# Moving the rare tiles' branch, the split of gathered tiles and two small turns in a convolution, attention and expert kernel

## The chip, the cores and the metric

The kernel runs on one core of a Trainium2 chip. The metric is the device time of one execution in microseconds; lower is better. A profile of one execution tells what each engine did: TensorE (PE, with its weight loads as PEld), VectorE (DVE), ScalarE (ACT), GpSimd (POOL) and SyncE (SP), which only issues transfers here. A letter q behind an engine's name (PEldq, POOLq) means its instruction queue: register loads, branches, semaphore instructions.

## The reference, cut to what matters

Two layers on an image of 256 channels and 48 x 48 pixels, 2304 tokens:

```python
x = x + _L0_conv_ref(_gn(x), ...)         # group norm, q, k, v, full softmax attention over 4 * 2304 rows
t = _to_tokens(x)                         # 2304 tokens of 256 channels
t = t + _L1_attn_ref(_ln_t(t), ...)       # attention over 64 slices
t = t + _L1_ffn_ref(_ln_t(t), ...)        # experts, below
x = _from_tokens(t, x)

def _L1_ffn_ref(x, Wg, bg, W1, b1, W2, b2):
    gate_logits = xf @ Wg + bg
    top_w, top_i = jax.lax.top_k(gate_logits, 2)
    top_w = jax.nn.softmax(top_w, axis=-1)
    w_dense = ...                          # weight of each of 8 experts for each token, two of them not zero
    for e in range(8):
        h = jax.nn.gelu(xf @ W1[e] + b1[e], approximate=False)   # 256 -> 1024
        out = out + w_dense[:, e:e + 1] * (h @ W2[e] + b2[e])    # 1024 -> 256
    return out
```

All of it is float32.

## The kernel before, in words

The first layer opens with the weights' turns, the group norm and the projections (lines 247 to 360); its attention over 9216 rows takes most of the time, up to about 1215 us. The change doesn't touch it. Two places are touched: the first 17 us, and the expert stage from about 1278 us on.

**The start.** Weights are turned on TensorE into PSUM tiles `pw` (two of them in turn, pool `ps_w`) and copied out by ScalarE. VectorE computes mean and variance of the channels; TensorE spreads them over groups with a small matrix (`gm`) into a PSUM tile `pgb`. `busy_first(n)` issues n matmuls without a use[...]; they write another part of the same tile `pgb`. `spread()` issues the second group matmul (the variance) and turns all biases (`brow`, 78 rows) into `pb`, which is a part of `pgb` again. VectorE then copies `pb` to `bcol` and scales the query's bias to `bq8`. The norm of five blocks of tokens (TBLOCKS) and their projections follow (`pq`, `pk` from a pool of five PSUM tiles `pp`).

**Routing.** The gate gives each token two experts. The (token, expert) pairs are sorted by expert into tiles of 128 rows: 36 tiles are always there (`SURE`), up to 7 more by how the experts' counts are rounded up: tiles 36 to 38 are "near" ones, 39 to 42 (from `FAR` on) are "rare" ones. `slot_t` holds for each tile the row of each slot, `part_t` the same for quarters of rows. `used_i` is the number of tiles in use. For the inputs here tiles 36, 37 and 38 run, and no rare tile does: 39 tiles of work are in the profile (1248 matmuls `ph`, 32 a tile). At the end of routing `busy(8, spin)` issues eight fillers on TensorE.

**A tile's work.** GpSimd gathers its 128 rows from memory with an indirect transfer: whole rows (`rows`, one transfer, into `xs`) or in four parts of 64 columns (`parts`, four transfers). A tile in rows is turned by TensorE and copied by VectorE (`turn`); a tile in parts needs no TensorE, VectorE turns it in two instructions (`turn_parts`). `first(s)` multiplies by W1 (32 matmuls into PSUM tiles `ph`, three in turn) and ScalarE puts Gelu into `hid`. `second(s)` multiplies by W2 (16 matmuls into `py`), VectorE adds the bias and scales by the token's weight (`y`), and `scatter(s)` adds the rows to `t_d` in memory, again by GpSimd. SyncE loads W1 of the tile's expert, 1 MB (`load_w1`, two buffers). All of W2 stays on the chip. In the trace `w` is W1 and `w_sb` W2.

**Order.** The order on each engine is made when the kernel is built: a scheduler takes what its model holds ready, in the order of the program. An `If` is one block: what stands inside is not mixed with what stands outside. In the program's order:

1. gathers of the near tiles and of tiles 0 and 1, W1 of tiles 36 and 37;
2. the value `used` is loaded on every engine, and the nested `If`s of the rare tiles (lines 1350 and 1355) follow; all are jumped over here;
3. tile 36, then tiles 37 and 38, each in an `If` (line 1386) that is entered here;
4. the loop over the 36 sure tiles: first(s), gather and load of tile s + 2, second(s - 1) with the turn of tile s + 1 in its middle, scatter(s - 1). At s = 4 `judge` computes whether the attention's sums stayed in range (its flag decides at the end whether everything runs again), with a turn on TensorE into `pm`.
5. the last sure tile isn't scattered, but added while the result is turned and stored.

Where an `If` is jumped over, each engine runs a few semaphore instructions that stand in for what was left out.

Lines that matter: `spread` (293), `busy(8, spin)` (1202), `ring_xs` (1220), `in_parts` (1254), `parts` (1257), `turn` (1278), the rare tiles (1354 to 1360), `judge` (1367), the near tiles (1382 to 1392), the loop (1395 to 1420).

Of the kernel before, what the change touches and what calls it, by code (L numbers as in the profile page):

```python
# [9 lines left out]
FP = mybir.dt.float32  # L10
# [55 lines left out]
def layers(  # L66
# [181 lines left out]
    with proj, tc.tile_pool(name="ps_pj", bufs=5, space=PSUM) as ps_pj, tc.tile_pool(  # L248
# [11 lines left out]
            nc.scalar.copy(dst, pw)  # L260
            return dst

        pgb = ps_g.tile([P, 512], FP, name="pgb")

        def busy_first(n):
            for _ in range(n):
                pe.matmul(
                    pgb[:, 256:512], ones, ones.unsqueeze(1).to_broadcast([P, 2, P]), start=True, stop=True
                )

        busy_first(14)
        WqT = transposed(pj.tile([P, 2, C], FP, name="WqT"), raws["Wq"])
        pg = pgb[:, 0:4].rearrange("p (a b) -> p a b", a=2)
        pb = pgb[:, 16:94]

        st = pj.tile([P, 2, 6, 6], FP, name="st")
        mv = pj.tile([P, 2, 2], FP, name="mv")
# [12 lines left out]
        mean = pj.tile([P, 2], FP, name="mean")  # L290
        dve.tensor_copy(mean, pg[:, 0, :])

        def spread():
            pe.matmul(pg[:, 1, :], gm, dm, start=True, stop=True)
            pe.transpose(pb, brow, ident[0:78, 0:78])

        busy_first(2)
        spread()
        WkT = transposed(pj.tile([P, 2, C], FP, name="WkT"), raws["Wk"])
        rstd = pj.tile([P, 2], FP, name="rstd")  # L300
        rsqrt(rstd, pg[:, 1, :], 1e-5, 2)
        xn = t_flat[:, 0 : 2 * NT].rearrange("p (c n) -> p c n", c=2)
        dve.tensor_copy(bcol, pb)
        bq8 = pj.tile([P, 2], FP, name="bq8")
        dve.tensor_scalar(bq8, bcol[:, B_Q : B_Q + 2], 0.125, None, ALU.mult)
        WvT = transposed(pj.tile([P, 2, C], FP, name="WvT"), raws["Wv"])

        for bi, (t0, tn) in enumerate(TBLOCKS):
            toks = slice(t0, t0 + tn)
            for c in range(2):  # L310
                nc.vector.tensor_scalar(
                    xn[:, c, toks], x_sb[:, c, toks], mean[:, c : c + 1], rstd[:, c : c + 1],
                    ALU.subtract, ALU.mult,
                )
            for m in range(2):
                cols = slice(m * P, (m + 1) * P)
                pq = ps_pj.tile([P, 512], FP, name="pp", tag="pp")
                pk = ps_pj.tile([P, 512], FP, name="pp", tag="pp")
                for c in range(2):
                    nc.tensor.matmul(  # L320
                        pq[:, 0:tn], WqT[:, c, cols], xn[:, c, toks], start=(c == 0), stop=(c == 1)
                    )
# [727 lines left out]
    with gating, tc.tile_pool(name="onehot", bufs=1) as oh, tc.tile_pool(  # L1050
# [148 lines left out]
                pq[:, k, :], quad[:, k, :, :].rearrange("p q s -> p (q s)"), empties, start=True, stop=True,  # L1199
            )  # L1200
        dve.tensor_scalar(part_t, pq, 4.0, quarter, ALU.mult, ALU.add)
        busy(8, spin)

    def expert_of(s, engine):
        return nc.values_load(
# [5 lines left out]
    with tc.tile_pool(name="ps_h", bufs=1, space=PSUM) as ps_h, tc.tile_pool(  # L1211
# [5 lines left out]
        def ring(pool, n, shape, name):  # L1217
            return cycle([pool.tile(shape, FP, name=f"{name}{k}") for k in range(n)])

        ring_xs, ring_w1 = ring(fp, 2, [P, C], "xs"), ring(fp, 2, [P, 2, HID], "w1")  # L1220
        ring_xT, ring_hid = ring(fp, 3, [P, 2, P], "xT"), ring(fp, 2, [P, NHC, P], "hid")
        ring_y = ring(fp, 2, [P, C], "y")
        ring_ph, ring_py = ring(ps_h, 3, [P, 4, P], "ph"), ring(ps_y, 2, [P, C], "py")
# [2 lines left out]
        near_xs = iter([fp.tile([P, C], FP, name=f"near_xs{s}") for s in range(SURE, FAR)])  # L1226
        fin = ctx.enter_context(tc.tile_pool(name="fin", bufs=1))
        far_xs, far_w1 = fin.tile([P, C], FP, name="far_xs"), fin.tile([P, 2, HID], FP, name="far_w1")
        here = fin.tile([P, NT], FP, name="here")
        held = fin.tile([P, NTT], FP, name="held")  # L1230
        obs = cycle([fin.tile([P, 2, 512], FP, name=f"ob{k}") for k in range(3)])
# [20 lines left out]
            return xs  # L1252

        def in_parts(s):
            return 2 <= s < SURE and s % 4 != 1

        def parts(s, xs):

# [16 lines left out]
            )  # L1275
            return w1

        def turn(xs):

            pt = next(ring_pt)  # L1280
            for c in range(2):
                pe.transpose(pt[:, c, :], xs.rearrange("p (d c) -> p c d", c=2)[:, c], ident)
            xT = next(ring_xT)
            dve.tensor_copy(xT, pt)
            return xT

# [7 lines left out]
                )  # L1294
            return xT

        def first(s, xT, w1):

            e = expert_of(s, mybir.EngineType.Activation)
            hid = next(ring_hid)  # L1300
# [12 lines left out]
            return hid  # L1313
# [32 lines left out]
            xs[s] = rows(s, next(near_xs))  # L1346
        for s in range(2):
            w1[SURE + s] = load_w1(SURE + s, next(ring_w1))
            xs[s] = parts(s, next(ring_xs))
        used = nc.values_load(  # L1350
            used_i, min_val=0, max_val=NSL,
            skip_runtime_bounds_check_because="it is a sum of counts, cut at NSL",
        )

        with ExitStack() as more:
            for s in range(FAR, NSL):
                more.enter_context(tc.If(used > s))
                issued.clear()
                far = turn(rows(s, far_xs))
                scatter(s, second(s, first(s, far, load_w1(s, far_w1)), lambda: None))  # L1360
        issued.clear()

        def turn_next(s):
            if s in xs:
                xT[s] = (turn_parts if in_parts(s) else turn)(xs.pop(s))
# [1 line left out]
        def judge():  # L1367

            both = fp.tile([P, 2], FP, name="both", tag="judge")
            dve.tensor_reduce(both, ends_of, AX.X, ALU.max)  # L1370
            dve.tensor_scalar(both[:, 0:1], both[:, 0:1], HIGH, None, ALU.is_gt)
            dve.tensor_scalar(both[:, 1:2], both[:, 1:2], 1.0 / LOW, None, ALU.is_gt)
            dve.tensor_tensor(both[:, 0:1], both[:, 0:1], both[:, 1:2], ALU.max)
            pm = ps_j.tile([1, P], FP, name="pm")
            pe.transpose(pm, both[:, 0:1], ident)
            dve.tensor_reduce(bad, pm, AX.X, ALU.max)
# [6 lines left out]
        hid[SURE] = first(SURE, xT.pop(SURE), w1.pop(SURE))  # L1383
        w1[SURE + 2] = load_w1(SURE + 2, next(ring_w1))
        scatter(SURE, second(SURE, hid.pop(SURE), more_turns))
        with ExitStack() as more:
            for s in near[1:]:
                more.enter_context(tc.If(used > s))
                issued.clear()
                hid[s] = first(s, xT.pop(s), w1.pop(s))  # L1390
                scatter(s, second(s, hid.pop(s), lambda: turn_next(s + 1) if s + 1 in near else None))
        issued.clear()
        for s in range(2):
            w1[s] = load_w1(s, next(ring_w1))
        for s in range(SURE):
            hid[s] = first(s, xT.pop(s), w1.pop(s))
            if s + 2 < SURE:
                xs[s + 2], w1[s + 2] = parts(s + 2, next(ring_xs)), load_w1(s + 2, next(ring_w1))
            if s == 0:
                turn_next(1)  # L1400
            elif s < SURE - 2:
                scatter(s - 1, second(s - 1, hid.pop(s - 1), lambda: turn_next(s + 1)))
            if SURE - 3 <= s < SURE - 1:

                scatter(s, second(s, hid.pop(s), lambda: turn_next(s + 1) if s == SURE - 2 else None))
            if s == 4 and bad is not None:
                judge()
            if s == 6:
                dve.tensor_scalar(
                    held, lim[:, 0:NTT], -1.0, empties[:, SURE - 1 : SURE], ALU.mult, ALU.add  # L1410
# [105 lines left out]
```

## Time and profile before

| what | value |
|---|---|
| time, three runs | 1590.86 us median (1588.08, 1590.86, 1597.04) |
| the profiled execution | 1584.99 us |
| its span, first to last instruction | 1583.3 us |
| mean granted TensorE clock | 0.997 |
| gathers in parts | 104 issues (26 tiles of 4), 1.01 us each on GpSimd |
| gathers in rows | 10 issues for sure tiles, 3 for near ones |
| scatters | 38 issues, 1.62 us each |
| W1 of one tile | 3.57 us on the chain of waits |
| W2 of one tile | 3.46 us |
| copies `xT<-pt` behind a TensorE turn | 13, 0.42 us each |

How to read it: "busy" is the time in which an engine executes; a wait is the idle time in front of an instruction, put down to what ended last before it. On TensorE a matmul in float32 is recorded as two instructions, and the recorded ends of neighbouring matmuls overlap, so distances between starts are taken for the time of a group. The time of an instruction on GpSimd's row is the time to issue a transfer; the data land later. Stretches list for each engine the busy time, and the granted clock of TensorE (1.00 is full speed).

### The profile page before, as it was taken

Reading aid. Unit: us, or ns where it says so; the run is one execution under the profiler, and the core shown is the slowest. Engines: PE = TensorE matmul, PEld = TensorE weight load, DVE = VectorE, ACT = ScalarE, POOL = GpSimd, SP = SyncE. Lnnn points to the kernel's source line nnn. Section 1 sums busy time; section 2 is a strip of 40 time slices with the busy share of each in tenths; the row PEclk is TensorE's granted clock in tenths of the full one; section 3 lists DMA queues with packets and bytes.
Section 4 is the critical chain, followed back from the end, with each engine's and each line's share of the span. In section 5 each row is a group of like instructions: output and inputs, shape, how many; then the busy total and the mean of one; then the engine's idle time right before and its main releaser. Section 6 shows DMA issues by size and latency. Waiting matters only on the chain. (4 is left out here: it accounts for less than half of the span.)

```text
span 1583.3 us, 32306 instructions
## 1 busy us (share of the span) xinstructions
PE 1562.8 (99%) x13105; PEld 781.2 (49%) x13105; DVE 1038.1 (66%) x1323; ACT 830.9 (52%) x1168; POOL 270.0 (17%) x210
## 2 busy tenths in 40 slices
PE   9999999999999999999999999999999999999998
PEld 5633343333333333333333333333334689999996
DVE  7578787787777778878778778787787731211111
ACT  2256565565666556656656566566655433333331
POOL 0001001011010010110101101101010135767671
PEclk9999999999999999999999999999999999999999
DMA  4000000000000000000000000000000946666665
GB/s 137 1 1 1 1 1 3 7 1 1 9 1 1 8 1 2 7 2 2 4 5 1 2 8 1 1 8 1 1 2 14 337 141 194 195 185 183 190 180 162
DMA packets 53071, 79.32 MB, mean 50 GB/s; under 512 B 22719, under 2 KB 43406, under 8 KB 47790
## 3 DMA queue, kind: packets, MB, share of 16 engines
q1 hardware_dynamic: 42834, 66.45, 12.7%
q0 software_dynamic: 9424, 10.10, 3.7%
q8 instruction: 108, 1.77, 0.4%
q10 hardware_dynamic: 652, 0.56, 0.1%
q14 instruction: 53, 0.43, 0.1%
HBM read 62.94 MB, written 12.32 MB: 48 GB/s over the span
## 5 line engine op out<-in xcount | busy, mean ns | idle before, releaser
L60 ACT ACTIVATE p<-s 128x1024 f32<-128x1024 f32 x648 | 663.3, 1024 | 470.4 <-PE s L60 465.2
L60 DVE TENSOR_TENSOR acc<-acc,p 128x1024 f32<-128x1024 f32 x612 | 749.3, 1224 | 243.4 <-ACT p L60 237.4
L60 PE MATMUL av<-p,v_sb 64*64 64x512 f32 x5184 | 675.7, 590 | 2.4 <-ACT p L60 1.3
L60 PE MATMUL s<-q,kk 64*64 64x512 f32 x5184 | 674.7, 589 | 0.5 <-DVE tn L60 0.5
L60 PEld LDWEIGHTS s<-q,kk 64*64 64x64 f32 x5184 | 202.0, 133 | 353.6 <-issue 181.5
L60 PEld LDWEIGHTS av<-p,v_sb 64*64 64x64 f32 x5184 | 195.6, 131 | 357.9 <-ACT p L60 201.0
L60 POOL PARTITION_ALL_REDUCE total<-both x17 | 71.1, 4185 | 1011.5 <-ACT p L60 833.6
L60 ACT ACTIVATE hid<-ph,bcol 128x128 f32<-128x128 f32 x312 | 89.3, 368 | 197.5 <-PE ph L60 185.2
L60 PEld LDWEIGHTS ph<-xT,w 128*128 128x128 f32 x1248 | 146.9, 194 | 2.7 <-issue 0.7
L60 PE MATMUL ph<-xT,w 128*128 128x128 f32 x1248 | 147.3, 277 | 0.6 <-issue 0.6
L60 PE MATMUL py<-w_sb,hid 128*128 x624 | 142.8, 379 | 0.0
L60 PEld LDWEIGHTS py<-w_sb,hid 128*128 128x128 f32 x624 | 114.9, 190 | 13.6
L1237 POOL DMA_INDIRECT xs<-tn_d,part_t x104 | 106.2, 1021 | 39.2 <-issue 30.8
L60 DVE TENSOR_TENSOR y<-py,b_bc 128x256 f32<-128x256 f32 x39 | 16.6, 425 | 126.2 <-PE py L60 126.2
L1237 POOL DMA_INDIRECT t_d<-y,slot_t x38 | 61.6, 1620 | 56.9 <-DVE y L60 37.9
L60 DVE STREAM_TRANSPOSE xT<-xs 128x128 f32<-128x128 f32 x52 | 13.1, 290 | 51.0 <-DMA xs<-tn_d,part_t 51.0
L60 DVE COPY xT<-pt 128x256 f32<-128x256 f32 x13 | 5.4, 424 | 53.1 <-PE pt L60 53.1
L60 DVE RECIPROCAL rinv<-rinv 128x256 f32<-128x256 f32 x17 | 29.7, 1745 | 0.0
L60 POOL TENSOR_TENSOR rstd_t<-ve,mhalf 128x2 f32<-128x2 f32 (+2 forms) x13 | 11.0, 849 | 102.8 <-DVE ve L60 96.0
L60 DVE TENSOR_TENSOR acc<-p 128x1024 f32<-128x1024 f32 x18 | 22.1, 1225 | 4.9 <-ACT p L60 3.3
L337 DVE TENSOR_SCALAR q<-pp,bcol 64x512 f32<-64x512 f32 (+1 forms) x30 | 20.8, 694 | 6.2 <-PE pp L320 5.8
L60 DVE TENSOR_REDUCE up<-av 128x512 f32<-128x1024 f32 x17 | 20.8, 1225 | 5.0 <-PE av L60 5.0
(302 smaller groups left out, 620.4 us busy)
## 6 DMA issues: line engine op xcount, KB each, us to landing
w<-in_L_ffn_W_dram SPq DMA_DIRECT2D x39, 1024.0 KB, 6.5
w_sb<-in_L_ffn_W_dram SPq DMA_DIRECT2D x8, 1024.0 KB, 10.2
t_sb<-turned SPq DMA_DIRECT2D x224, 8.0 KB, 1.8
x_sb<-in_x_dram SPq DMA_DIRECT2D x3, 576.0 KB, 3.8
xs<-tn_d,part_t POOLq DMA_INDIRECT x104
t_d<-t_sb SPq DMA_DIRECT2D x2, 768.0 KB, 10.7
tn_d<-tn SPq DMA_DIRECT2D x2, 768.0 KB, 5.7
t_sb<-t_d SPq DMA_DIRECT2D x3, 512.0 KB, 4.6
```

What stands on the lines that cost most here:

```text
L60: return self.tc.keep_in_program_order(getattr(self.engine, name)(*args, **kwargs))
L337: nc.vector.tensor_scalar(dst, pq[rows, 0:tn], bcol[rows, B_Q + m : B_Q + m + 1], 0.125, ALU.add, ALU.mult,)
L1237: new = nc.gpsimd.indirect_dma_start(**kwargs)
```

## The change

In neutral words:

- Start: the fillers get a PSUM tile of their own (`spun`, one of the five `pp`), `pgb` shrinks to 96 columns; the turn of the biases, the copy `bcol` and `bq8` move from before the norm to behind the norm of the first block, into a `pw` tile.
- The fillers at the end of routing go from 8 to 6.
- Tiles in parts: s % 3 < 2 instead of s % 4 != 1, for 2 <= s < 36.
- `ring_xs` has three buffers instead of two; tiles 0, 1 and 2 are gathered ahead, and the loop gathers tile s + 3. Tiles are turned two ahead (s + 2): a TensorE turn in the middle of second(s - 1), a turn in parts behind it, before the scatter.
- The rare tiles' nested `If`s move from before tile 36 into the loop, behind second(0) and scatter(0) at s = 1; they get `hid` and `xT` tiles of their own. The load of `used` moves behind tile 36.
- `judge` is split: VectorE's part stays at s = 4, the turn and the flag (`verdict`) come at s = 5.

```diff
-        pgb = ps_g.tile([P, 512], FP, name="pgb")
+        pgb = ps_g.tile([P, 96], FP, name="pgb")
+        spun = ps_pj.tile([P, 512], FP, name="pp", tag="pp")
...
                 pe.matmul(
-                    pgb[:, 256:512], ones, ones.unsqueeze(1).to_broadcast([P, 2, P]), start=True, stop=True
+                    spun[:, 0:256], ones, ones.unsqueeze(1).to_broadcast([P, 2, P]), start=True, stop=True
                 )
...
-        def spread():
-            pe.matmul(pg[:, 1, :], gm, dm, start=True, stop=True)
-            pe.transpose(pb, brow, ident[0:78, 0:78])
-
         busy_first(2)
-        spread()
+        pe.matmul(pg[:, 1, :], gm, dm, start=True, stop=True)
...
-        dve.tensor_copy(bcol, pb)
         bq8 = pj.tile([P, 2], FP, name="bq8")
-        dve.tensor_scalar(bq8, bcol[:, B_Q : B_Q + 2], 0.125, None, ALU.mult)
...
+        def biases():
+            pb = ps_w.tile([P, 512], FP, name="pw", tag="pw")
+            pe.transpose(pb[:, 0:78], brow, ident[0:78, 0:78])
+            nc.vector.tensor_copy(bcol, pb[:, 0:78])
+            nc.vector.tensor_scalar(bq8, bcol[:, B_Q : B_Q + 2], 0.125, None, ALU.mult)
...
+            if bi == 0:
+                biases()
...
-        busy(8, spin)
+        busy(6, spin)
...
-        ring_xs, ring_w1 = ring(fp, 2, [P, C], "xs"), ring(fp, 2, [P, 2, HID], "w1")
+        ring_xs, ring_w1 = ring(fp, 3, [P, C], "xs"), ring(fp, 2, [P, 2, HID], "w1")
...
+        far_hid = fin.tile([P, NHC, P], FP, name="far_hid")
+        far_xT = fin.tile([P, 2, P], FP, name="far_xT")
...
         def in_parts(s):
-            return 2 <= s < SURE and s % 4 != 1
+            return 2 <= s < SURE and s % 3 < 2
...
         for s in range(2):
             w1[SURE + s] = load_w1(SURE + s, next(ring_w1))
+        for s in range(3):
             xs[s] = parts(s, next(ring_xs))
-        used = nc.values_load(
...
-        with ExitStack() as more:
-            for s in range(FAR, NSL):
-                more.enter_context(tc.If(used > s))
-                issued.clear()
-                far = turn(rows(s, far_xs))
-                scatter(s, second(s, first(s, far, load_w1(s, far_w1)), lambda: None))
-        issued.clear()
...
         scatter(SURE, second(SURE, hid.pop(SURE), more_turns))
+        used = nc.values_load(
...
+        def rare():
+            with ExitStack() as more:
+                for s in range(FAR, NSL):
+                    more.enter_context(tc.If(used > s))
+                    issued.clear()
+                    far = turn(rows(s, far_xs), far_xT)
+                    scatter(s, second(s, first(s, far, load_w1(s, far_w1), far_hid), lambda: None))
+            issued.clear()
...
         for s in range(SURE):
             hid[s] = first(s, xT.pop(s), w1.pop(s))
-            if s + 2 < SURE:
-                xs[s + 2], w1[s + 2] = parts(s + 2, next(ring_xs)), load_w1(s + 2, next(ring_w1))
             if s == 0:
                 turn_next(1)
-            elif s < SURE - 2:
-                scatter(s - 1, second(s - 1, hid.pop(s - 1), lambda: turn_next(s + 1)))
+            if s + 3 < SURE:
+                xs[s + 3] = parts(s + 3, next(ring_xs))
+            if s + 2 < SURE:
+                w1[s + 2] = load_w1(s + 2, next(ring_w1))
+            if 0 < s < SURE - 2:
+                ahead = None if in_parts(s + 2) else s + 2
+                y = second(s - 1, hid.pop(s - 1), lambda: turn_next(ahead))
+                turn_next(s + 2)
+                scatter(s - 1, y)
+                if s == 1:
+                    rare()
+            elif s == 0:
+                turn_next(2)
             if SURE - 3 <= s < SURE - 1:
-                scatter(s, second(s, hid.pop(s), lambda: turn_next(s + 1) if s == SURE - 2 else None))
+                scatter(s, second(s, hid.pop(s), lambda: None))
             if s == 4 and bad is not None:
-                judge()
+                both = judge()
+            if s == 5 and bad is not None:
+                verdict(both)
```

More of the change, by code (lines that the diff above doesn't have):

```diff
@@ L273, in layers @@
         pg = pgb[:, 0:4].rearrange("p (a b) -> p a b", a=2)
-        pb = pgb[:, 16:94]
         st = pj.tile([P, 2, 6, 6], FP, name="st")
@@ L1276, in load_w1, with turn @@
             return w1
-        def turn(xs):
+        def turn(xs, xT=None):
             pt = next(ring_pt)
@@ L1282, in turn @@
                 pe.transpose(pt[:, c, :], xs.rearrange("p (d c) -> p c d", c=2)[:, c], ident)
-            xT = next(ring_xT)
+            xT = next(ring_xT) if xT is None else xT
             dve.tensor_copy(xT, pt)
@@ L1295, in turn_parts, with first @@
             return xT
-        def first(s, xT, w1):
+        def first(s, xT, w1, hid=None):
             e = expert_of(s, mybir.EngineType.Activation)
-            hid = next(ring_hid)
+            hid = next(ring_hid) if hid is None else hid
             for f0 in range(0, NHC, 4):
@@ L1348, in layers @@
             w1[SURE + s] = load_w1(SURE + s, next(ring_w1))
+        for s in range(3):
             xs[s] = parts(s, next(ring_xs))
-        used = nc.values_load(
[L1351 to L1355, printed above, removed]
-            for s in range(FAR, NSL):
-                more.enter_context(tc.If(used > s))
-                issued.clear()
-                far = turn(rows(s, far_xs))
-                scatter(s, second(s, first(s, far, load_w1(s, far_w1)), lambda: None))
-        issued.clear()
         def turn_next(s):
@@ L1373, in judge, with verdict @@
             dve.tensor_tensor(both[:, 0:1], both[:, 0:1], both[:, 1:2], ALU.max)
+            return both
+        def verdict(both):
             pm = ps_j.tile([1, P], FP, name="pm")
@@ L1385, in layers @@
         scatter(SURE, second(SURE, hid.pop(SURE), more_turns))
+        used = nc.values_load(
+            used_i, min_val=0, max_val=NSL,
+            skip_runtime_bounds_check_because="it is a sum of counts, cut at NSL",
+        )
         with ExitStack() as more:
```

## The prediction

> **What bounds the kernel now.** I read the page first, for the shares, then TensorE's waits from 1276 us on (that is where most of the diff lies), then the branch's own line, the timeline and the stretches around it, and at last the first 20 us.
>
> The page's first part:
> ```profile
> PE 1562.8 (99%) x13105; PEld 781.2 (49%) x13105; DVE 1038.1 (66%) x1323; ACT 830.9 (52%) x1168; POOL 270.0 (17%) x210
> ```
> TensorE is busy 1562.8 of 1583.3 us, so only some 20 us can be won by removing waits, and every matmul that is added costs its own time. TensorE's waits after 1276 us:
> ```profile
> PE pt L60 <- PEq L1355: 1.5, 1, 1.5
> PE ph L60 <- DMA t_sb<-t_d: 0.7, 2, 0.5
> PE ph L60 <- issue: 0.6, 1, 0.6
> ```
> In the whole expert stage there is one wait that the change can touch: 1.5 us in front of the first turn of tokens, released by TensorE's own queue at the branch over the rare tiles. No gather and no scatter ever stops TensorE before the tail. The instructions of the branch's line:
> ```profile
> L1355 POOLq EVENT_SEMAPHORE  x4: 17/42/43, 1286.5 to 1286.7; - x4
> L1355 PEldq EVENT_SEMAPHORE  x2: 51/51/51, 1283.4 to 1283.5; - x2
> L1355 PEldq COMPARE_BRANCH  x1: 4209/4209/4209, 1279.1 to 1279.1; - x1
> L1355 DVEq COMPARE_BRANCH  x1: 72/72/72, 1279.5 to 1279.5; - x1
> L1355 POOLq COMPARE_BRANCH  x1: 53/53/53, 1280.3 to 1280.3; - x1
> ```
> The jump takes 4.2 us on TensorE and under 0.1 us elsewhere; GpSimd is then held until 1286.5, when its last gather has landed. The timeline there:
> ```profile
> 1277.82 1.38 POOL L1237 DMA_INDIRECT near_xs<-tn_d,slot_t  x1 [22.27 <-DVE slot_w L60]
> 1278.55 3.70 PE L60 MATMUL spin<-Wqkv_sb,ident 128*128 128x256 f32 x16
> 1283.76 0.47 PE L60 MATMUL pt<-ident,near_xs 128*128 128x128 f32 x2 [1.50 <-PEq L1355]
> 1284.79 5.44 PE L60 MATMUL ph<-xT,w 128*128 128x128 f32 x32 [0.56 <-issue]
> ```
> The 16 filler matmuls (busy(8)) end at 1282.25, the turn starts at 1283.76, and the first tile's W1 takes 5.44 us where every later one takes 3.57 to 3.73. Why, the stretches show (columns: busy PE, PEld, DVE, ACT, POOL, then granted clock, DMA share, GB/s):
> ```profile
> 1282.25:1283.73 1.48, 0.00 (x1) 0.00 (x1) 0.00 (x0) 0.00 (x0) 1.18 (x2) 1.00 0.31 91
> 1284.79:1288.37 3.58, 3.58 (x18) 3.58 (x19) 0.00 (x0) 0.00 (x0) 0.00 (x0) 0.54 0.12 37
> ```
> After the idle stretch the clock is halved for 3.4 us. Two chain and register lines of the steady loop, for the branch's new place:
> ```profile
> 1322.84 3.46 PE py L60 x16
> ...
> L60 PEldq FUSED_REGOPS  x2: 55/55/55, 1322.0 to 1322.3; - x2
> ```
> The last of the eight address computations of a tile's W2 runs at 1322.2, with W2 itself ending at 1326.30: the queue runs about 3.9 us ahead of the array. The start, four lines:
> ```profile
> 11.07 0.35 PE L60 MATMUL pgb<-mv,gmat 128*128 128x2 f32 x2
> ...
> 12.12 2.08 PE L60 MATMUL pgb<-ones 128*128 128x256 f32 x4 [0.70 <-DVE mean L60]
> ...
> 14.69 0.16 DVE L60 TENSOR_SCALAR ve<-pgb 128x2 f32<-128x2 f32 x1 [2.62 <-PE pgb L60]
> ...
> 16.30 1.98 PE L320 MATMUL pp<-t_sb,WqT 128*128 128x512 f32 x4 [0.38 <-DVE t_sb L311]
> ```
> The fillers share a bank with the mean, and wait 0.70 us until VectorE has copied it; the variance then stands behind them.
>
> [...]
>
> **The change part by part**, against the profiled execution (1584.99 us, span 1583.3; the median of the runs shown, 1590.86, lies 5.87 above).
>
> 1. *Branch out of its place, fillers 8 to 6.* Four fillers of 0.23 us go (3.70/16), so they end at 1278.55 + 12 x 0.231 = 1281.32. The turn needs the first rare-near gather: issued 1277.82 to 1279.20; the sixteen arrivals on its semaphore end at 1281.34 in the trace. So the turn starts at about 1281.5 and not 1283.76: -2.26 us. If the gather is late by 1 us, -1.3. What is late next is VectorE's copy (the 0.56 us), which stays.
> 2. *Clock.* The idle stretch shrinks to about 0.2 + 0.56 us, and the first W1 should run at full speed: 3.57 for 5.44, -1.87. [...] I take -1.87 for the profiled one.
> 3. *Branch in its new place*, after W2 of tile 0. From the branch (1279.0) to the turn (1283.76) is 4.75 us; the queue's lead is 3.88 us there (1326.29 - 1322.41, the last dispatch being one step of 0.22 after 1322.2). So 0.87 us of idle comes back. At best the join itself remains, some 0.45 us (the two semaphore instructions and dispatch, 1283.31 to 1283.76); with a lead of only 2.1 us, as when W2's last piece waits for Gelu (branch on L1386 at 1306.3, W2 over at 1308.4), 2.65. I take +0.87, without a clock drop: 1.41 us of idle at 1226 to 1228 had none. On the other engines: ScalarE and VectorE join when their own last work is done, which is before TensorE needs them (Gelu has 3.5 us of slack, W2 of the tile before). GpSimd waits for all its gathers and the scatter to land: the scatter lands 3.8 us after issue (1557.68 to 1561.49), so GpSimd loses about 2.5 us once; the following gathers have 7 us more lead than before and cover it. The load of "used" moves behind the first near tile (0.49 us on TensorE's queue), under a lead of 2.65 us: nothing; 0.5 if that cover is gone. SP's loads of W1 aren't held: at 1270.1 to 1270.5 its join passed with two loads in flight.
> 4. *In parts two of three.* PE turns are for tiles s % 3 == 2 from 2 to 35, twelve, where s % 4 == 1 gave eight. A tile with a PE turn takes 7.26 us between W1 starts, one without 7.03 (matmul steps 3.57 + 3.46): +0.23 each, 4 x 0.225 = +0.90. It lies on TensorE, with nothing beside it. It removes four times three issues of 1.31 us from GpSimd, which was not the bound: from 1300 to 1550 TensorE never waits.
> 5. *Gathers three ahead, turns two ahead.* xT is ready 2.1 to 4.2 us before W1 in parts, 1.5 us with a PE turn. No wait, so nothing to win in this execution: 0. If other executions have later gathers, see rival B.
> 6. *Check's turn later.* It and its wait add 14.39 - 2 x 7.03 - 0.225 = 0.1 us; the turn stays, so 0 to -0.1: -0.05.
> 7. *Start.* Without the wait the fillers start at 11.42 (-0.70), and the bias turn (0.16) leaves the front of the two weight turns. Statistics reach VectorE at about 13.8 instead of 14.69, the norm ends at about 15.3 (16.25 before). But TensorE is then still at the last weight turn, half clocked until 15.3, and takes the bias turn of 0.2 to 0.3 us: first projection at about 15.55. -0.75; at least -0.4 if the bias turn waits for ScalarE's copy, at most -0.95. Behind it TensorE is busy, so it counts in full. The two bias operations (0.23 + 0.16) move behind the first norm, before 18.5 where they are used.
>
> Sum: -2.26 - 1.87 + 0.87 + 0.90 - 0.05 - 0.75 = -3.16: span 1580.1, execution 1581.8, and on the median 1587.7.
>
> **Rivals.**
> A. *The stall only moves, clock and all* (or the clock loss was not in most executions): part 2 gives nothing: -1.3, 1589.6. [...] Against: less idle in a row.
> B. *Gathers are late in the runs not profiled.* These took 3 to 12 us more than the profiled one, and the smallest slack is 2.1 us. If that is TensorE waiting for tokens, seven more microseconds of lead take most of it: 1582. For it: three tiles in parts in a row cost GpSimd 7.15 us each (4 x 1.31 + 1.9) against 7.03. Against: a fourth tile lets it catch up, and this trace shows no wait.
> C. *Slower.* At the new place the lead is short, because the scheduler leaves W2's last pieces behind a late Gelu: idle 4.75 - 2.1 = 2.65, and clock loss of 1.87 comes with it: -2.26 - 1.87 + 2.65 + 1.87 + 0.90 - 0.05 - 0.75 = +0.5, 1591.4. It decides from 4.0 us of idle and clock loss together at that branch (the other terms' sum). For it: all three near branches run at leads of 2.1 to 2.7. Against: in the loop Gelu of the tile before is long done.
>
> **How the numbers follow.** The forecast has 0.56, A 0.16, B 0.18, C 0.10. Its own terms reach from -5.0 (all best) to -0.5, and runs of this kernel scatter by 9 us, so a median of few may be off by 3 or 4: 1582 to 1592. B pulls the low end to 1580.5, C the high one to 1592.5. About 0.5% (8 us) can be told from no change: faster than 1582.9 takes most of B and a tail of the forecast, 0.29; slower than 1598.8 only scatter and C's worse forms, 0.06; the rest 0.65.
>
> **What would show it.** Right: no wait at L1355 before the first turn, which starts near 1281; the first W1 in 3.6 us at clock 1.00; a long COMPARE_BRANCH on TensorE's queue after tile 0's W2 with about 0.9 us of idle; 17 copies xT<-pt for 13; first projection near 15.5 us. Wrong: idle over 2 us or a halved clock at that branch, TensorE waiting for xs in the loop, or a gain that none of these places holds.

## The result, and the profile after

In the comparison of the two kernels the one before took 1592.37 us (median of 18 runs, 1587.33 to 1597.04) and the one after 1583.94 us (18 runs, 1582.48 to 1587.37): a ratio of 0.9949, 95% interval 0.9939 to 0.9958, or 8.1 us less. The two profiled executions differ by much less: 1584.99 us before, 1583.29 us after, spans 1583.3 and 1581.6. The profile shown of before is an execution quicker than any of its 18 timed ones. So there are two questions: do the 1.7 us between the profiles come from where the sum put them, and where do the other six come from? A warning ahead: by signs that the experiments show (under the third chip), the profile of before was taken on one kind of chip and that of after on another, so their difference is not the change's alone.

The page of after, its first part:

```profile
PE 1560.0 (99%) x13109; PEld 778.0 (49%) x13109; DVE 1035.6 (65%) x1319; ACT 830.7 (53%) x1168; POOL 257.9 (16%) x198
```

TensorE is still the bound, and GpSimd has 12 instructions fewer, as the split says. Next, its TensorE waits from 1276 us to the end (us in total, times, longest):

```profile
PE ph L60 <- DVE y L60: 0.9, 1, 0.9
PE pt L60 <- DMA xs<-tn_d,slot_t: 0.7, 2, 0.5
PE ph L60 <- DMA t_sb<-t_d: 0.6, 2, 0.5
PE ph L60 <- issue: 0.5, 1, 0.5
PE py L60 <- ACT hid L60: 0.2, 1, 0.2
```

The 1.5 us at the branch before the first turn are gone. In their place stand 0.9 us at the branch's new place and 0.7 us for row gathers, a wait that the kernel before did not have. The line of the branch in its new place, after tile 0's W2:

```profile
L1395 POOLq EVENT_SEMAPHORE  x4: 17/43/4435, 1315.8 to 1320.4; - x4
...
L1395 PEldq COMPARE_BRANCH  x1: 3934/3934/3934, 1310.5 to 1310.5; - x1
...
L1395 POOLq INC_SWDGE_SEM  x1: 566/566/566, 1320.5 to 1320.5; - x1
```

TensorE's jump still takes 3.9 us, nearly all of it hidden under W2; GpSimd stands at its join (the semaphore instructions behind a jump) until what it has issued has landed, 4.4 + 0.6 us (the last arrival of the scatter issued at 1315.50 is recorded at 1320.31, and the wait ends at 1320.34). The timeline at the two places:

```profile
1276.83 2.84 PE L60 MATMUL spin<-Wqkv_sb,ident 128*128 128x256 f32 x12
...
1279.50 0.39 PE L60 MATMUL pt<-ident,near_xs 128*128 128x128 f32 x2
...
1280.41 3.84 PE L60 MATMUL ph<-xT,w 128*128 128x128 f32 x32 [0.52 <-issue]
...
1314.94 3.81 PE L60 MATMUL ph<-xT,w 128*128 128x128 f32 x32 [0.86 <-DVE y L60]
```

The turn follows the 12 fillers at once, and the first W1 takes 3.84 us, not 5.44. The "DVE y" at 1314.94 is a label only: W1 doesn't read y. What ends last before it is the queue's own join, at 1314.5 and 1314.7, behind the branch that ended at 1314.4. The start:

```profile
11.34 1.11 PE L60 MATMUL pp<-ones 128*128 128x256 f32 x4
...
12.60 0.16 DVE L60 TENSOR_SCALAR ve<-pgb 128x2 f32<-128x2 f32 x1 [0.48 <-PE pgb L60]
...
14.22 1.13 PE L322 MATMUL pp<-t_sb,WqT 128*128 128x512 f32 x2 [0.72 <-DVE t_sb L311]
```

The fillers no longer wait for the mean and run at full speed (1.11 us for four, 2.08 before), the variance reaches VectorE at 12.60 and not 14.69, and the first projection starts 2.08 us earlier.

The difference of the profiles can be laid out by distances on TensorE's line (start of one group to start of the next; minus is a gain):

| stretch | before | after | difference |
|---|---|---|---|
| to the fillers (spin) | 1278.55 | 1276.83 | -1.72 |
| fillers to first turn (pt) | 5.21 | 2.67 | -2.54 |
| first turn to first W1 | 1.03 | 0.91 | -0.12 |
| first W1 to second | 9.20 | 7.60 | -1.60 |
| second W1 to last | 262.40 | 266.23 | +3.83 |
| the rest of the span | | | +0.45 |

These add to -1.70. The +3.83 is the split's four turns and the branch, and some two microseconds more that no term of the sum held: two steps (from one tile's W1 to the next) of 7.71 and 8.06 us where 7.26 is the rule, and one of 7.69.

### The profile page after: what moved, and what is told of

The parts are those of the page before. It is cut to its first block, busy times and chain, and to the rows that moved or that the text cites. A ratio compares the mean times of both kernels' runs of the same rounds, so it can differ in the third digit from the quotient of the medians.

```text
span 1581.6 us, 32250 instructions
## 1 busy us (share of the span) xinstructions
PE 1560.0 (99%) x13109; PEld 778.0 (49%) x13109; DVE 1035.6 (65%) x1319; ACT 830.7 (53%) x1168; POOL 257.9 (16%) x198
## 5 line engine op out<-in xcount | busy, mean ns | idle before, releaser
L1241 POOL DMA_INDIRECT xs<-tn_d,part_t x88 | 90.2, 1025 | 29.9 <-issue 25.6
L1241 POOL DMA_INDIRECT t_d<-y,slot_t x38 | 61.3, 1613 | 77.2 <-DVE xT L60 30.3
L60 PE MATMUL spin<-Wqkv_sb,ident 128*128 128x256 f32 x82 | 19.2, 382 | 0.0
```

The source lines that it names most:

```text
L60: return self.tc.keep_in_program_order(getattr(self.engine, name)(*args, **kwargs))
L1241: new = nc.gpsimd.indirect_dma_start(**kwargs)
```

## The experiments

The theory put to the test is the sum: every part is worth what its place on TensorE's line shows. The rival is B's: the timed runs of before lose time in the loop that its profile doesn't show, and either earlier gathers or less work for GpSimd takes it away. Each set of runs stood on one chip, beside the kernel before on that chip, and the chip turned out to matter.

**First chip: one part at a time.** The kernel before again, unchanged:

> The kernel before, unchanged, profiled in another execution. Its timed runs lie 2.3 to 12 us above the one profiled execution (1584.99), so that one was a lucky draw. Theory 'late gathers' (rival B): this profile shows TensorE waiting for xs or xT between 1300 and 1550, several us in all, and W1 starts further apart than 7.03 or 7.26. Theory 'clock and branch': no such waits, the loop keeps its steps, and what is longer lies before the loop: more stretches of 3.4 us at half clock (1.7 us each), at the start and at the branch.

The start alone:

```
-        pgb = ps_g.tile([P, 512], FP, name="pgb")
+        pgb = ps_g.tile([P, 96], FP, name="pgb")
+        spun = ps_pj.tile([P, 512], FP, name="pp", tag="pp")
...
+            if bi == 0:
+                biases()
```

> Only the start is changed (own tile for the fillers, biases behind the norm). By the prediction's sum -0.75; by the trace of the changed kernel -2.1 (first projection at 14.2 instead of 16.3), part of it the half clock that fell there. 'Late gathers': no more than that, -0.8 to -2.1. If most of the 8 us is here, -5 or more, both are wrong.

The branch alone, with the fillers at 6 and the load of "used" behind the first near tile:

```
-        busy(8, spin)
+        busy(6, spin)
...
+                if s == 1:
+                    rare()
```

> Only the branch is moved (with the load of the count behind the first near tile, own tiles for the rare ones) and the fillers cut to 6. By the prediction's sum -2.26 - 1.87 + 0.87 = -3.3. 'Late gathers': the same or worse, since GpSimd is held some 5 us at the new place while gathers are only two ahead: -3.3 to +1. 'Clock and branch': -4 to -6, if typical runs lose more than the profiled one at the old place.

The split and the gathers three ahead together:

```
-            return 2 <= s < SURE and s % 4 != 1
+            return 2 <= s < SURE and s % 3 < 2
...
+            if s + 3 < SURE:
+                xs[s + 3] = parts(s + 3, next(ring_xs))
```

> Only the gathers are changed (two of three tiles in parts, three buffers, gathered three and turned two ahead); branch, start and check stay. By the prediction's sum +0.9 for four more turns on TensorE. 'Late gathers': -3 to -7, most of what the sum doesn't explain.

| run | median us | runs | ratio to before | interval |
|---|---|---|---|---|
| before, beside them | 1584.58 | 46 | | |
| before_again | 1584.56 | 12 | 1.0002 | 0.9994 to 1.0010 |
| start_only | 1583.57 | 21 | 0.9991 | 0.9985 to 0.9998 |
| branch_only | 1587.62 | 9 | 1.0021 | 1.0011 to 1.0030 |
| gather_only | 1585.54 | 13 | 1.0005 | 0.9997 to 1.0013 |

On this chip the kernel before takes 1584.6 us, not 1592. In before_again every W1 of the steady loop, but for the step with the check, starts 7.03 or 7.26 us after the one before it. The half clock of its first W1 isn't there either (first step 7.57 us): it fell at 1228.4. The start is worth about 1 us; its first projection is at 14.31, against 15.34 in before_again, where the fillers ran at full clock (1.13 us). Split and gathers together cost 1.0 us (the interval holds nothing too). The branch alone costs 3.0 us. Its TensorE waits from 1276 to 1566:

```profile
PE ph L60 <- DVE xT L60: 2.9, 3, 2.2
PE ph L60 <- DVE y L60: 1.0, 1, 1.0
PE py L60 <- DVEq L1389: 0.3, 1, 0.3
```

The second line is the branch, 1.0 us. The first is new: W1 waits for turned tokens, 2.2 us of it in one step, which takes 9.43 us. By the author's reading that is GpSimd's stand at the join (4.4 + 0.6 us in after), which with gathers only two tiles ahead comes through to TensorE some ten tiles later: the gathers' lead falls to 3.0 us at tile 11, from 5.6 in before. So on this chip the branch's move loses by itself. That a longer lead covers it is seen in the whole change only, below.

**Second chip: one part left out at a time.** The kernel before (one execution), the kernel after again, and the kernel after without the split, and without the branch's move and its fillers:

> The kernel before once more, one look, to have its trace from the chip of this series. If the chip is like that of the last series (before at 1584.6), the loop keeps its steps of 7.03 and 7.26 with no wait for xs or xT. If it is like that of the first times (before at 1592), 'late gathers' says that TensorE's waits for xT stand in the loop, 5 to 8 us in all; 'clock and branch' says none, and more half clock.

> The whole change, unchanged. 'The sum' with what the last series measured (start -1.4, gathers +1.0, branch -3.3 if the gathers are far enough ahead to cover GpSimd's stop): -3 to -4 where before takes 1584.6. 'Late gathers': -8 where before takes 1592, and about -3 where it takes 1584.6; the gain is the larger the slower the chip's gathers are. If the parts simply add as measured alone (-1.4 + 3.3 + 1.0): +2.9, slower.

```
-            return 2 <= s < SURE and s % 3 < 2
+            return 2 <= s < SURE and s % 4 != 1
```

> The whole change but for the split: three of four tiles stay in parts (s % 4 != 1). 'The sum': four turns of 0.225 us less on TensorE, so 0.9 below the whole change. 'Late gathers': GpSimd is loaded more and the stop at the branch costs it 5 us, so waits for xT come back: 0 to +4 against the whole change.

```
-                if s == 1:
-                    rare()
...
-        busy(6, spin)
+        busy(8, spin)
```

> The whole change but for the branch and the fillers: both stay in front of the first tile. 'The sum': 2.4 to 4.3 above the whole change (the stall of 1.5 with its four fillers, and the half clock[...], against 0.87 at the new place). 'Late gathers': the same or less, since GpSimd isn't stopped in the loop.

| run | median us | runs | ratio to before | interval |
|---|---|---|---|---|
| before, beside them | 1592.37 | 29 | | |
| before_look | 1594.88 | 1 | | |
| after_again | 1584.52 | 6 | 0.9954 | 0.9937 to 0.9970 |
| all_but_modulo | 1590.79 | 14 | 0.9991 | 0.9978 to 1.0004 |
| all_but_branch | 1587.29 | 16 | 0.9961 | 0.9946 to 0.9975 |

This chip gives the first comparison again, and here the split, which costs 0.9 us of TensorE's own time, is worth 6.3 us beside the longer lead (1590.79 - 1584.52), the branch with its fillers 2.8. What is different on it, before_look shows. Its distance from first to last W1 is 280.76 us, against 271.60 in the profile shown of before and 269.96 in before_again. Eight steps of its loop are 7.31 to 9.29 us long where 7.03 and 7.26 are the rule. The worst of them on TensorE:

```profile
1473.36 3.22 PE L60 MATMUL ph<-xT,w 128*128 128x128 f32 x18
1477.62 1.75 PE L60 MATMUL ph<-xT,w 128*128 128x128 f32 x14 [1.03 <-issue]
```

and the stretch around it (columns: busy PE, PEld, DVE, ACT, POOL, then granted clock, DMA share, GB/s), beside a W1 of the same run that isn't disturbed:

```profile
1473.30:1479.10 5.80, 4.50 (x34) 3.96 (x33) 0.78 (x2) 2.61 (x10) 3.10 (x4) 1.00 0.47 157
1482.60:1486.20 3.60, 3.60 (x34) 3.57 (x33) 0.78 (x2) 1.14 (x4) 0.31 (x1) 1.00 0.64 200
```

The same W1 is stretched from 3.6 to 5.8 us in the middle of its group, at full clock, and with less DMA traffic than the undisturbed one; the matmul behind the longest gap, 1.03 us, waits for nothing that the profile shows. So rival B as it was written, TensorE waiting for xs or xT, is little of what is seen: 1.1 of the 9.2 us that this loop is longer. The timeline of VectorE there, in before_look:

```profile
1477.87 0.42 DVE L60 TENSOR_TENSOR y<-py,b_bc 128x256 f32<-128x256 f32 x1 [5.79 <-remote]
```

It adds the bias to the W2 that TensorE finished at 1473.5. In the profile shown of before it starts 0.20 us after that W1 does (1467.93 and 1468.13); here 4.5 us after (1473.36 and 1477.87), and its releaser is one the trace cannot name. So it isn't TensorE alone that stands: VectorE does too, and ScalarE has gaps of 1.79 and 1.40 us in the same stretch. What else differs is GpSimd. Its waits from 1300 to 1550 us, in before_again on the first chip:

```profile
POOL t_d L1237 <- DVE y L60: 33.8, 17, 3.8
...
POOL t_d L1237 <- issue: 14.5, 14, 5.4
```

and in before_look on this one:

```profile
POOL t_d L1237 <- DVE y L60: 29.7, 13, 5.5
POOL t_d L1237 <- DMA t_d<-y,slot_t: 17.2, 5, 4.0
```

In before_again no scatter waits for an earlier scatter to land; here five do, for 17.2 us. Much of that is a new name for an old wait: one of the five waits 4.01 us for a landing at 1455.41, where the same scatter of before waited 3.62 us for y. And the first chip has such waits too, 5.2 us once in gather_only and 10.4 us in two in branch_only, with no W1 stretched in gather_only. What is longer here is GpSimd's distance from TensorE: the gathers beside the W1 at 1473.36 begin 1.5 us ahead of it, at 1471.87, where in before they begin 3.6 us ahead (1464.35 and 1467.93). GpSimd is 2.1 us further behind, at the third tile in parts in a row, where by an estimate from the traces' issue times (4 x 1.31 + 1.9 = 7.15 us a tile, in a step of 7.03) it has no time to catch up.

Is this lag the cause? Where it sets in, the order of events is in the trace. In before_look that is at tile 9, 24 us before the first stretched group of the loop (a lag at tile 4 passes at once):

```profile
1384.15 3.73 PE L60 MATMUL ph<-xT,w 128*128 128x128 f32 x32
...
1384.75 1.01 POOL L1237 DMA_INDIRECT xs<-tn_d,part_t  x1 [0.30 <-issue]
1386.71 0.42 DVE L60 TENSOR_TENSOR y<-py,b_bc 128x256 f32<-128x256 f32 x1 [4.22 <-PE ph L60]
...
1387.80 1.82 POOL L1237 DMA_INDIRECT t_d<-y,slot_t  x1 [2.04 <-DVE y L60]
```

and the same tile in the profile shown of before:

```profile
1383.12 0.42 DVE L60 TENSOR_TENSOR y<-py,b_bc 128x256 f32<-128x256 f32 x1 [2.27 <-PE py L60]
...
1383.51 1.01 POOL L1237 DMA_INDIRECT xs<-tn_d,part_t  x1 [0.30 <-issue]
```

There W1 starts at 1382.92. GpSimd's gather comes 0.6 us after W1 in both, so it isn't late yet; y comes 2.56 us after W1 and not 0.20, and only then does the scatter wait for it, 2.04 us. In modulo_only, ahead_only, all_but_branch, after and after_again, too, the first late y finds GpSimd in step. So the lag begins as an effect of the late y. Whether it adds to what follows isn't shown.

All_but_modulo, with the denser split, has the stretched W1s again: four steps of 9.25, 9.55, 7.47 and 9.90 us in its loop, each four tiles after the one before, which is the period of its split, and 284.21 us from first to last W1. Its window around the branch also shows what rival C described:

```profile
1308.00:1324.00 16.00, 14.15 (x97) 13.42 (x96) 2.03 (x7) 5.72 (x20) 8.37 (x7) 0.89 0.59 169
```

1.8 us of idle at the join, then the clock halved at 1320.5 for 3.4 us (the mean is 0.89), and two steps of 8.18 and 8.73 us.

**Third chip: the split alone, the lead alone, and less in parts.** The edits are the two shown for gather_only, one at a time in the kernel before, and this in the kernel after:

```
-            return 2 <= s < SURE and s % 3 < 2
+            return 2 <= s < SURE and s % 2 == 0
```

> The kernel before, with two of three tiles in parts in place of three of four, and nothing else. The sum of the prediction: four more TensorE turns of 0.225 us, so +0.9 us on any chip. GpSimd's load: where the kernel before loses time inside the groups of its loop (W1 starts up to 9.3 us apart instead of 7.03 or 7.26, as in the look before), the third tile in parts in a row is what brings it, and the split alone takes most of it away: -5 to -7 us, with no W1 distance over 8 us in the loop. Late gathers: the split helps only as far as xT comes earlier; about -2. Where the kernel before loses nothing in its loop, all three say +0.9 us.

> The kernel before, with gathers three tiles ahead and turns two ahead, the split left at three of four. The sum: 0 us. Late gathers: where the kernel before loses time in its loop, one tile (7 us) more lead takes it away, -5 to -7 us. GpSimd's load: the gathers are as many and as dense as before, so the losses inside the groups stay, 0 us within 1, with W1 distances over 8 us at some third tile in parts.

> The kernel after, with every second tile in parts in place of two of three: 17 tiles in parts of s = 2 to 34, 17 with a TensorE turn where the kernel after has 12. The sum: five more turns of 0.225 us, +1.1 us against the kernel after, so about -0.3 us from the start, branch and clock terms and the six to nine turns against the kernel before where its loop loses nothing. GpSimd's load: the same +1.1 against the kernel after, if two of three has removed all that the load costs; below +0.5, or a gain, if the second tile in parts in a row still costs something. Late gathers: as the sum, since three ahead has already covered them.

| run | median us | runs | lowest to highest | ratio to before | interval |
|---|---|---|---|---|---|
| before, beside them | 1592.33 | 38 | 1585.31 to 1600.12 | | |
| modulo_only | 1591.29 | 14 | 1585.98 to 1596.10 | 0.9993 | 0.9976 to 1.0010 |
| ahead_only | 1594.00 | 22 | 1590.09 to 1598.49 | 1.0009 | 0.9999 to 1.0020 |
| half_parts | 1585.35 | 9 | 1584.46 to 1585.97 | 0.9959 | 0.9946 to 0.9972 |

A chip like the second, and neither theory of a single part holds: the split alone gains nothing that can be told, the lead alone nothing either. With both (and the start) all_but_branch came to 0.9961, some 6 us on the second chip, of which the start is worth about 1. So on such chips the two parts are worth some 5 us together, an estimate, for they were never timed there without the start, and about nothing apart. The traces hint at what each one lacks. In ahead_only one step of 8.95 us has a W1 stretched in its middle, as in before_look. In modulo_only the longest step of the loop, 8.36 us, is TensorE waiting in front of a turn for gathered rows, which is rival B's own symptom. And both kernels end with a long wait. TensorE's waits of modulo_only from 1555 us, the last tokens read back from memory:

```profile
PE ph L60 <- DMA t_sb<-t_d: 2.3, 2, 1.9
```

It is 2.1 us in ahead_only, 0.7 in before and 0.2 in half_parts. This tail costs more than the wait: in modulo_only the clock is halved at 1570.8 for 3.4 us behind it, and both kernels take 30.3 to 30.4 us from the last W1 to the end of the span, where all others take 26.8 to 28.1.

Half_parts has calm runs: 1.5 us from lowest to highest, where before has 14.8. It was not run beside the kernel after; by their ratios to before (0.9959; 0.9949 and 0.9954) the two are equal within the intervals, so the 1.1 us of its five more turns and a possible gain from the lighter load can't be told apart.

What makes y late stands in the traces' records of semaphores, the counters by which one engine tells another that it is done. In before_look the last five signals of the W2 before 1477.87 belong to matmuls that end at 1471.80 to 1473.53; they are recorded at 1477.68 to 1477.85, y starts at 1477.87, and the stretched W1 goes on at 1477.62. The two other long stops inside a W1 of this trace end, at 1416.73 and 1447.07, within 0.1 us of five such signals as well. So VectorE isn't slow there: the signal that it waits for comes late, and TensorE's stop ends as its signals go out. TensorE has 228 to 269 signals between 1300 and 1550 us. In the table, a late one is recorded more than 0.06 us away from the end of any matmul that sends one:

| traces | tiles in parts | late signals |
|---|---|---|
| before, before_again, start_only, branch_only, gather_only, gather_again (below) | 26 or 22 | 0, and 1 in branch_only |
| all_but_modulo, before_look, ahead_only | 26 | 84, 85, 96 |
| after, all_but_branch, modulo_only, after_again | 22 | 66, 67, 68, 74 |
| half_parts | 17 | 33 |

The first row is the profile shown of before and the two chips where the kernel before takes about 1585 us, the quiet kind; the other rows are the two chips where it takes 1592, and the profile shown of after. On the second kind the number of late signals falls with the number of tiles in parts, so with GpSimd's gathers, and not with the lead. Few late signals alone don't save time, as modulo_only shows; all kernels there that save it have the lead as well. What holds the signals isn't shown. The traces of the second kind also hold fewer landings of transfers (1098 in that stretch of before_look, 2804 in before, the same kernel), so their labels "remote", "issue" and "DMA t_d" may hide a releaser that wasn't recorded. The pages show it: the one of before has a time to landing for W1, the one of after has none.

```profile
w<-in_L_ffn_W_dram SPq DMA_DIRECT2D x39, 1024.0 KB, 6.5
...
w<-in_L_ffn_W_dram SPq DMA_DIRECT2D x39, 1024.0 KB
```

**Fourth chip: split and lead together once more**, to see their 5 us without the start's edit:

> The kernel before with the split and the gathers three ahead together, start, branch and fillers as before. The same kernel as the run gather_only, to be read beside the kernel before on this chip. The sum: +0.9 us on any chip. If the loss in the loop needs both parts to go (neither alone took it away), and this chip shows it (before near 1592 us): -4 to -6 us, with loop steps of 7.03 and 7.26 us throughout. If the chip has no such loss (before near 1584.5 us): +0.9 us again, and the question stays open. If it has the loss and this kernel gains nothing: the loss goes only with the branch's or the start's edit, and the split isn't what removes it.

The kernel before took 1585.56 us on this chip (17 runs) and gather_again 1585.74 (13 runs), 1.0002 (0.9994 to 1.0011). This is a chip without the loss, and the run couldn't answer the question. It repeats the other answer: its trace has 272.63 us from first to last W1, as gather_only on the first chip has to the hundredth; with the same half-clocked first step (9.20) the kernel before has 271.60. So the split costs 1.03 us there, and the lead has nothing to give.

The whole change was never timed on a chip of the quiet kind, so what it gains there is open. The 1.7 us of the two profiles don't tell, since the two come from different kinds. The parts measured alone would add to a loss of some 3 us (-1.0 + 3.0 + 1.0), but the branch's late gathers (2.9 us) need not come with three tiles of lead: in after, tiles 6 to 16 are gathered as far ahead of their W1 as in gather_only, which has no branch in its loop (from the end of the last gather's issue to W1: 13.12 and 13.10 us for tile 12), where branch_only falls to 3.0 us at tile 11 from 5.6 in before.

## Why the prediction came out as it did

The time, 1583.94 us, lies inside the range and 3.8 us below the number given. Most steps were right by mechanism. That the number is so near is in part luck: the loop's loss, which is most of the gain, had no term in the sum, and the range reached to 1580.5 only for rival B.

1. *Branch out, fillers 8 to 6*: -2.26 predicted, -2.54 measured (fillers to first turn). The first gather had been issued 1.7 us earlier with all the rest, so nothing was late.
2. *Clock*: -1.87 predicted, -1.60 measured in the pair of profiles. But before_again and start_only show the first W1 at full clock with the branch in its old place (first step 7.57 us in before_again). The gain belongs to executions in which the half clock fell there, as rival A said. In half_parts and all_but_modulo, with the branch moved, the first step is 9.31 and 9.23 us long all the same, at full clock. The place of the half clock changes from one execution to the next: the 3.4 us of half clock stand at 11.9 and 1285.0 in one execution of the kernel before, at 1228.4 in another, at 1228.6 and 1286.6 in a third. The idle before it was 1.5 and 0.56 us before 1285.0, and 1.41 us before 1228.4. What sets its place isn't shown.
3. *Branch in its new place*: +0.87 predicted, 0.86 measured. The method, branch time less the queue's lead, holds. (The trace has the branch's start at 1279.08, not 1279.0, and the first gather's last arrival at 1281.41, not 1281.34; neither moves a term by 0.1 us.) Of the sentence "GpSimd loses about 2.5 us once; the following gathers have 7 us more lead than before and cover it" the size failed and the cover held. GpSimd loses 5.2 us (1315.84 to about 1321.0): the estimate took a landing 3.8 us after the scatter's issue, where this one came 4.8 us after it (1315.50 to 1320.31), and left out the join's own 566 ns. The gathers up to tile 16 don't show it. The two row gathers that come late, by 0.2 and 0.5 us, are those of tiles 20 and 23, behind a late y at tile 12; with their steps of 7.71 and 8.06 us (+1.25) they belong to the kind of chip. And "without a clock drop: 1.41 us of idle at 1226 to 1228 had none" is no reason: the same 1.41 us of idle is followed by half clock at 1228.4 in before_again and at 1228.6 in before_look. So why after and after_again lost no clock at the branch isn't explained by it.
4. *In parts two of three*: +0.90 predicted, 1.03 by the traces of gather_only and gather_again. Right in size as TensorE work; but the step added that GpSimd "was not the bound", and so left its relief at nothing. On the second chip that relief, together with the lead, is worth more than the turns cost: after_again is 6.3 us quicker than all_but_modulo.
5. *Gathers three ahead*: "No wait, so nothing to win in this execution: 0". True of the execution, and of the chips like it. This is the step that failed for the median: the number was set against a median 5.87 us above the profiled execution without asking what those 5.87 us were made of. By the signs above the profile is of the one kind of chip and the median of the other. Rival B asked; it had the gain's size (1582) and its cure right, more lead with less work for GpSimd, and its symptom mostly wrong: but for 1.1 us TensorE isn't seen waiting for tokens in before_look, it stands inside its groups.
6. *Check's turn*: -0.05, too small to be seen in any run; not tried alone.
7. *Start*: -0.75 predicted, -2.08 in the pair of profiles, of which 1.72 still stand at 1276. Beside it -1.03 in start_only against before_again, and 1.0 us in time. The sum took the half-clocked weight turns as fixed ("half clocked until 15.3"), but the half clock at 11.9 was that execution's own; in before_again and before_look the fillers ran in 1.13 us. For those the term was about right.

What rival C described, idle at the branch with a clock loss behind it, is seen in all_but_modulo: 1.8 us of idle, then 3.4 us at half clock. In after and after_again it isn't: 0.9 and 0.7 us of idle, and full clock behind it. The jump is hidden about as well in both kernels (it starts 0.4 us before tile 0's W2 in after, 0.7 us in all_but_modulo), but from its end to the next W1 pass 0.5 us in the one and 1.4 in the other.

So the sum of -3.16 met -1.70 in the profiles: the start gave 1 us more than priced, and the loop gave back some 2 us by late gathers, a second step of 7.69 us (7.77 in before_look too) and the tail. And it met -8.1 in the medians, since the kernel before loses time in its loop on the second kind of chip (9.2 us in before_look, its one trace), a loss that the profile shown doesn't have.

What stays open is what holds TensorE's signals on the second kind of chip, and whether recording the profile has a part in it. That the long stops inside W1 in before_look end as late signals go out, and that there are fewer of them with fewer tiles in parts, is shown; that the gathers cause them is argued from that order alone. The time on GpSimd's row doesn't tell when a scatter's data have landed: a scatter shows 1.62 us on average in before_again and in before_look, whether or not the next one then waits for it to land; the one of 1.62 us at 1315.50 in after lands 4.8 us after its issue.

## What to carry to other kernels

Before summing what an edit is worth, set the profiled execution beside the timed runs: if it is quicker than nearly all of them, the profile doesn't hold the loss that a median is made of, and a zero for "no wait in this trace" is a zero for that execution alone. Look then at an engine whose work per step is as long as the step (here GpSimd, an estimated 7.15 us in 7.03), even where nothing waits for it: more lead and less work were each worth nothing alone that could be told here, and an estimated 5 us together. When an engine stands and the profile names nothing that it waits for, look at when its own signals went out: in before_look the long stops inside W1 ended as late ones did. A jump over code that isn't run can be hidden under a long group of matmuls, all but 0.9 us of it here, if the other engines' joins, and what they hold in flight, are counted too.

## What the runs showed of the hardware

- The same kernel has a median of 1584.6 and 1585.6 us on two chips and of 1592.3 and 1592.4 on two others, with runs of before 15 to 17 us apart on the latter; a change is worth -0.5% on one kind, while its parts measure within 0.2% on the other.
- A W1 of 32 matmuls stretched from 3.6 to 5.8 us at full granted clock in before_look, on the second kind of chip, and went on as five of TensorE's signals went out, 4.3 to 5.9 us after the matmuls that send them. Such late signals were 33 to 96 of some 250 there, the more the more tiles were gathered in parts, and 0 or 1 on the first kind.
- The branch over the rare tiles, whose body isn't run, took TensorE 4.2 us at its old place (before) and 3.9 us at its new one (after, all_but_modulo), and under 0.1 us on each other engine; GpSimd's join behind it took 5.2 us in after, with a scatter just issued and five gathers before it.
